# Two tiles to a PSUM bank in the graph convolution and the down projection, and another order of the feed-forward groups

## The chip, the cores and the metric

The kernel runs on one NeuronCore of one Trainium2 chip. The metric is the device time of one execution in microseconds (us). The core has five engines that run side by side, each through its own queue in order: TensorE for matmuls (PE, and PEld for its weight loads), VectorE (DVE), ScalarE (ACT), GpSimd (POOL), and SyncE (SP), which here only issues DMAs. TensorE writes its results to PSUM, which has banks of 512 fp32 values in each of 128 partitions.

## The reference

The input `x` has 32 graphs of 512 nodes with 256 features each; `adj` has a 512 x 512 integer adjacency matrix per graph. Two layers follow, each a graph step and a feed-forward step with residuals. What the change touches is in layer 0:

```python
# graph step (xn = layernorm of x)
h = einsum('bnf,fu->bnu', xn, W_msg)
msg_sum = einsum('bij,biu->bju', a, h)
deg = sum(a, axis=1)
messages = where(deg > 0, msg_sum / maximum(deg, 1), 0)
x = x + relu(einsum('bnf,fu->bnu', xn, W_upd) + messages + bias)

# feed-forward step (xf = layernorm of x, one row per node)
t = max over d of (xf[:, d] + Wt[f, d]) + bt          # 1024 values f per row
trop = s * max_k(t * sl_cvx + of_cvx) + (1 - s) * min_k(t * sl_ccv + of_ccv)
classical = gelu(xf @ Wc + bc)
g = sigmoid(xf @ Wg + bg)
x = x + (g * trop + (1 - g) * classical) @ Wd + bd
```

Layer 1 is an attention over the graph with four heads and a second mixer; nothing in it is changed.

## The kernel before

Layer 0 is `layer0_sorted`. The 32 graphs are handled in four segments of eight. A segment has 8 x 512 = 4096 rows, 32 tiles of 128 rows.

**The graph convolution.** `conv_in(b)` loads a graph, casts its adjacency to floats on POOL (L384), normalizes and transposes it, and makes the messages `h`: for each of four tiles two matmuls into `ph` (L393) and an ACT copy of 256 columns (L395). `conv_out(b)` goes through the four tiles: two matmuls into `pu` (L408), a DVE add of the bias into `u` (L411), four matmuls of the adjacency with `h` into `pm` (L414), whose last column is the degree, then on DVE its maximum with 1, its reciprocal and the scaled sum into `u` (L418 to L420), the relu and residual into `keep` (L422) and the statistics of the next layer norm (L424, L425). Its second half, the tail, normalizes each tile on ACT and finds on DVE a bound, the eight largest values and their places (L439 to L441), counts how many values can matter, and stores rows and values to HBM (`rows_of`, L450).

**The order of rows.** `put_in_order(s)` ranks the 4096 rows of a segment by that count (DVE passes over up to 4096 columns, L493, and small matmuls). Rows with a like count come to lie in the same tile; tile n of a segment needs at most `CAPS[n]` of the 256 features: 24 for the first tile, 9, 7, 6, 5 for the next ones, down to 1 for the last nine.

**The feed-forward groups.** A segment is worked through in NG = 8 groups of four tiles; group g has tiles g, g + 8, g + 16 and g + 24, so group 0 holds the tile that needs 24 features and group 7 is the lightest. `sums(s, g)` gathers the rows of a group (L533), and for each tile gathers a row of `table` (1024 values) for the largest feature (L544) and one for every further feature up to the cap (L578, four buffers); DVE adds the feature's value and takes the maximum (L581, the "row pass", 128 x 1024). Over the caps of its tiles a group makes 27 such passes for g = 0, and 12, 10, 9, 7, 7, 7 and 5 for g = 1 to 7. `mixed(s, g)` runs over eight blocks of 128 outputs: matmuls for `cls` and `gate` (L601) with an ACT function each (L603), the transposed sums `tz` (L608), ACT and DVE passes for the bends of the piecewise function (L614, L615) and three DVE passes that apply the gate (L617 to L619). `down(s, g)` multiplies the result with `wd`: for each of four tiles eight matmuls into `po` (L628) and a DVE add into `xs` (L630), then the group is stored.

**What sets the order.** The functions are generators, and `woven` steps two of them in proportion to given counts. `feed_forwards` runs `mixed` of a group woven with `sums` of the next group; `down` of the group before is issued after the first block of `mixed`. The whole of it is woven with `all_convs`, which works ahead on the convolutions of later segments, and after the last segment on preparations of layer 1. `sums` doesn't begin before its segment is in order. A scheduler then places the instructions on each engine; within an engine they run in that order. The pool of PSUM tiles has four tags of two banks each. `ph`, `pu`, `pm`, `po` and the small matmuls of `put_in_order` share the tag `mm`: each takes the next of its two banks, and waits until the engine that read that bank last is done. Groups come in this order:

```python
groups = [(s, g) for s in range(len(x2s)) for g in reversed(range(NG))]
```

So in each segment the lightest group comes first and the heaviest last.

Of the kernel before, what the change touches and what calls it, by code (L numbers as in the profile page):

```python
# [8 lines left out]
F32 = mybir.dt.float32  # L9
# [4 lines left out]
ALU = mybir.AluOpType  # L14
# [4 lines left out]
P = 128  # L19
N = 512  # L20
D = 256
NT = N // P
DC = D // P
# [3 lines left out]
def deviation(nc, rs, var, eps):  # L27

    nc.gpsimd.tensor_add(rs, var, eps[:, 0:1].to_broadcast(rs.shape))
    nc.gpsimd.tensor_tensor(rs, rs, eps[:, 1:2].to_broadcast(rs.shape), ALU.pow)  # L30
# [66 lines left out]
def layer0_sorted(tc, ident, eps, x, adj, w, x2s, ranks, over, following):  # L97
# [6 lines left out]
    nc = tc.nc  # L104
# [4 lines left out]
    FC = FFN // P  # L109
# [5 lines left out]
    NG = ST // NT  # L115
# [11 lines left out]
    with ExitStack() as ctx:  # L127
        cst = ctx.enter_context(tc.tile_pool(name="c0", bufs=1))
        dr = ctx.enter_context(tc.tile_pool(name="d0", bufs=2, space=DRAM))
        ps = ctx.enter_context(tc.tile_pool(name="p0", bufs=2, space=PSUM))  # L130

        def const(name, shape, src):
            t = cst.tile(shape, F32, tag=name, name=name)
            nc.sync.dma_start(t, src)
            return t

        w_msg = const("w_msg", [P, DC, D], w["W_msg"].rearrange("(c p) u -> p c u", p=P))
        w_upd = const("w_upd", [P, DC, D], w["W_upd"].rearrange("(c p) u -> p c u", p=P))
        bias = const("bias", [P, D], w["bias"].partition_broadcast(P))
# [3 lines left out]
        wd = cst.tile([P, FC, D], F32, tag="wd", name="wd")  # L143
# [34 lines left out]
        sa = aside.enter_context(tc.tile_pool(name="sa", bufs=2, side="right"))  # L178
# [197 lines left out]
        def conv_in(b):  # L376

            xg = sa.tile([P, NT, D], F32, tag="x", name=f"x{b}")
            nc.sync.dma_start(xg, x[b].rearrange("(t p) d -> p t d", p=P))
            a = sa.tile([P, NT, N], F32, tag="adj", name=f"adj{b}", bufs=2)  # L380
            for t in range(NT):
                ai = sa.tile([P, N], I32, tag="adji", name=f"adji{b}_{t}", bufs=2)
                nc.sync.dma_start(ai, adj[b, t * P : (t + 1) * P, :])
                nc.gpsimd.tensor_copy(a[:, t, :], ai)  # L384
            x1T = sa.tile([P, DC, N], F32, tag="x1T", name=f"x1T{b}", bufs=2)
            layer_norm_T(nc, sa, ps, ident, eps, xg, x1T, f"a{b}", pool=True)
            yield
            h = sa.tile([P, NT, D + 1], F32, tag="h", name=f"h{b}", bufs=1)
            nc.gpsimd.memset(h[:, :, D : D + 1], 1.0)
            for t in range(NT):  # L390
                ph = ps.tile([P, N], F32, tag="mm", name=f"ph{b}_{t}")
                for c in range(DC):
                    nc.tensor.matmul(ph[:, :D], x1T[:, c, t * P : (t + 1) * P], w_msg[:, c, :],  # L393
                                     start=c == 0, stop=c == DC - 1)
                nc.scalar.copy(h[:, t, :D], ph[:, :D])  # L395
            held[b] = xg, a, x1T, h
            yield

        def conv_out(b, counts):


            xg, a, x1T, h = held.pop(b)
            keep = sa.tile([P, NT, RW], F32, tag="keep", name=f"keep{b}")
            mv = sa.tile([P, NT, 2], F32, tag="mv", name=f"mv{b}")
            for t in range(NT):
                pu = ps.tile([P, N], F32, tag="mm", name=f"pu{b}_{t}")
                for c in range(DC):
                    nc.tensor.matmul(pu[:, :D], x1T[:, c, t * P : (t + 1) * P], w_upd[:, c, :],  # L408
                                     start=c == 0, stop=c == DC - 1)
                u = sa.tile([P, D], F32, tag="upd", name=f"u{b}_{t}")  # L410
                nc.vector.tensor_add(u, pu[:, :D], bias)  # L411
                pm = ps.tile([P, N], F32, tag="mm", name=f"pm{b}_{t}")
                for i in range(NT):
                    nc.tensor.matmul(pm[:, : D + 1], a[:, i, t * P : (t + 1) * P], h[:, i, :],  # L414
                                     start=i == 0, stop=i == NT - 1)

                deg = sa.tile([P, 1], F32, tag="deg", name=f"deg{b}_{t}")
                nc.vector.tensor_scalar_max(deg, pm[:, D : D + 1], 1.0)  # L418
                nc.vector.reciprocal(deg, deg)
                nc.vector.scalar_tensor_tensor(u, pm[:, :D], deg, u, ALU.mult, ALU.add)  # L420
                x1 = keep[:, t, :D]
                nc.vector.scalar_tensor_tensor(x1, u, 0.0, xg[:, t, :], ALU.max, ALU.add)  # L422
                st = sa.tile([P, 6], F32, tag="ln_st", name=f"stb{b}_{t}", bufs=4)
                nc.vector.bn_stats(st, x1)  # L424
                nc.vector.bn_aggr(mv[:, t, :], st)  # L425
                yield
            rs = sa.tile([P, NT], F32, tag="ln_rs", name=f"rsb{b}", bufs=2)
            deviation(nc, rs, mv[:, :, 1], eps)
            shift = sa.tile([P, NT], F32, tag="ln_shift", name=f"shiftb{b}", bufs=2)
            nc.vector.scalar_tensor_tensor(shift, mv[:, :, 0], -1.0, rs, ALU.mult, ALU.mult)  # L430
            for t in range(NT):
                k, n = keep[:, t, :], b * NT + t
                nc.gpsimd.tensor_copy(k[:, MEAN : MEAN + 1], shift[:, t : t + 1])
                nc.gpsimd.tensor_copy(k[:, MEAN + 1 : MEAN + 2], rs[:, t : t + 1])
                xn = sa.tile([P, D], F32, tag="ln_xn", name=f"xnb{b}_{t}", bufs=3)
                nc.scalar.activation(xn, k[:, :D], AF.Identity, bias=shift[:, t : t + 1], scale=rs[:, t : t + 1])
                rest = sa.tile([P, D], F32, tag="rest", name=f"rest{n}")
                bound = ends[:, 0, n : n + 1]
                nc.vector.tensor_tensor_reduce(rest, xn, low, -1.0, 3e38, ALU.add, ALU.min, bound)  # L439
                nc.vector.max(k[:, VAL : VAL + 8], xn)  # L440
                nc.vector.max_index(k[:, IDX : IDX + 8].bitcast(U32), k[:, VAL : VAL + 8], xn)  # L441


                nc.scalar.activation(rest, xn, AF.Sign, bias=bound, accum_out=counts[:, t : t + 1])
                nc.gpsimd.tensor_copy(k[:, COUNT : COUNT + 1], counts[:, t : t + 1])
                nc.gpsimd.tensor_copy(ends[:, 1, n : n + 1], k[:, VAL : VAL + 1])
                if t + 1 < NT:
                    yield
            rows = rows_of[b // SEG].rearrange("(b t p) w -> b p t w", t=NT, p=P)
            nc.sync.dma_start(rows[b % SEG], keep)  # L450
            yield
# [61 lines left out]
        def convs(s):  # L513
            counts = sa.tile([P, ST], F32, tag="counts", name=f"counts{s}")
            yield from conv_in(s * SEG)
            for i in range(SEG):
                b = s * SEG + i
                after = conv_in(b + 1) if i + 1 < SEG else iter(())
                yield from woven(conv_out(b, counts[:, i * NT : (i + 1) * NT]), 8, after, 2)
            yield from put_in_order(s, counts)  # L520
            placed_segs.add(s)

        def feed_forwards():
# [98 lines left out]

            def down(s, g):
                xg, acc = got.pop((s, g))
                for t in range(NT):
                    po = ps.tile([P, N], F32, tag="mm", name=f"po{s}_{g}_{t}")
                    for f in range(FC):
                        nc.tensor.matmul(po[:, :D], acc[f][:, t * P : (t + 1) * P], wd[:, f, :],  # L628
                                         start=f == 0, stop=f == FC - 1)
                    nc.vector.tensor_add(xg[:, t, :D], xg[:, t, :D], po[:, :D])  # L630
                nc.sync.dma_start(x2s[s].rearrange("(t k p) d -> k p t d", k=NG, p=P)[g], xg[:, :, :D])

            got = {}
            groups = [(s, g) for s in range(len(x2s)) for g in reversed(range(NG))]
            yield from sums(*groups[0])
            for i, now in enumerate(groups):
                steps_ = mixed(*now)
                next(steps_)
                if i:
                    down(*groups[i - 1])  # L640
                yield
                more = sums(*groups[i + 1]) if i + 1 < len(groups) else iter(())
                yield from woven(steps_, 9, more, 8)
            down(*groups[-1])

        def all_convs():
# [20 lines left out]
        for _ in woven(feed_forwards(), NG * 11 + sum(1 + cap // 4 for cap in CAPS), ahead, SEG * 12 + 5):  # L667
            pass
# [1543 lines left out]
```

## Time and profile before

| | |
|---|---|
| time, median of 3 runs | 4689.87 us (4680.16 to 4715.24) |
| the profiled execution | 4695.45 us |
| its span in the profile | 4693.7 us, 56440 instructions |
| TensorE clock granted, mean share of full speed | 0.948 |
| row passes on DVE, L581 | 336, about 1.3 us each |
| down projections on PE, L628 | 456.2 us busy |
| DVE adds of a tile of 256 columns, L411, L630 | 413 ns and 411 ns, 128 of each |
| DVE residual pass of a tile, L422 | 441 ns, 128 of them |
| ACT copy of `h`, L395 | 373 ns, 128 of them |

The profile is one execution on the chip. A row of an engine's groups gives the line, the engine, the operation, what it writes and reads, the count, the busy time in us, the mean in ns, and then how long the engine was idle just before these instructions and what ended that wait. A row of waits says which instruction waited for which, with the total in us, how often, and the longest. A stretch of time is shown with its limits in us from the start of the span. A TensorE record covers part of a matmul only: two records stand for one fp32 matmul.

### The profile page before, as it was taken

To read this page: it belongs to the slowest core of one execution; us is meant where nothing else is said; L and a number is where in the kernel's file an instruction comes from. 1 tells how busy PE (TensorE), PEld (TensorE's weight loads), DVE (VectorE), ACT (ScalarE), POOL (GpSimd) and SP (SyncE) were. 2 spreads that over 40 slices of the span, in tenths; PEclk is the share of its full clock that TensorE was granted. 3 is DMA by queue.
4 is the path that set the end of the run, shared out by engine and by line. 5 is a ranking of instruction groups with operands and counts; after the bars stand their busy time and mean duration, and the time that the engine had idled before them with its cause. 6 is when DMAs were issued, how large, how long until landed. Compare 5 with 4: busy or idle time off the path is not lost. (4 is left out here: it accounts for less than half of the span.)

```text
span 4693.7 us, 56440 instructions
## 1 busy us (share of the span) xinstructions
PE 4097.9 (87%) x19287; PEld 2514.5 (54%) x19287; DVE 3410.9 (73%) x7232; ACT 2310.3 (49%) x4820; POOL 1747.3 (37%) x2027
## 2 busy tenths in 40 slices
PE   5769887889888899879988899999999999999987
PEld 4545554555555565545554355555555555555555
DVE  6667778777787777867777667777777777777773
ACT  2345555455554555546554444544454554444432
POOL 2363445535456444443443322233333233322220
PEclk8889999999999999989999899999999999999998
DMA  4453445535355343554443211111111111111100
GB/s 123 160 173 104 154 133 165 176 105 163 123 162 173 121 142 107 165 186 143 145 159 113 64 46 45 48 46 52 52 53 55 53 55 55 46 55 55 39 14 15
DMA packets 235101, 474.10 MB, mean 101 GB/s; under 512 B 38299, under 2 KB 114075, under 8 KB 234804
## 3 DMA queue, kind: packets, MB, share of 16 engines
q0 software_dynamic: 80256, 282.38, 19.0%
q1 hardware_dynamic: 154548, 188.02, 12.9%
q8 instruction: 154, 2.52, 0.2%
q14 instruction: 143, 1.17, 0.1%
HBM read 413.16 MB, written 57.16 MB: 100 GB/s over the span
## 5 line engine op out<-in xcount | busy, mean ns | idle before, releaser
L601 PE MATMUL clsp<-xnT,wc 128*128 128x512 f32 x1024 | 530.9, 639 | 92.7 <-ACT cls L603 48.5
L601 PE MATMUL gatep<-xnT,wg 128*128 128x512 f32 x1024 | 505.2, 615 | 32.9 <-ACT gate L603 23.4
L628 PE MATMUL po<-wd,acc 128*128 128x256 f32 x2048 | 456.2, 381 | 20.4 <-DVE xs L630 19.9
L628 PEld LDWEIGHTS po<-wd,acc 128*128 128x128 f32 x2048 | 385.9, 190 | 96.3 <-DVE xs L630 31.8
L1186 DVE SCALAR_TENSOR_TENSOR att<-own,other,mask 128x512 f32<-128x512 f32 x512 | 376.3, 757 | 17.9 <-DMA own<-ownd 16.9
L615 DVE SCALAR_TENSOR_TENSOR acc<-past,fld,acc 128x512 f32<-128x512 f32 x448 | 349.5, 784 | 51.7 <-ACT past L614 38.0
L581 DVE SCALAR_TENSOR_TENSOR best<-rows,xs,best 128x1024 f32<-128x1024 f32 x212 | 276.0, 1304 | 124.5 <-ACT best L575 62.5
L601 PEld LDWEIGHTS gatep<-xnT,wg 128*128 128x128 f32 x1024 | 200.3, 199 | 289.5 <-issue 210.6
L614 ACT ACTIVATE past<-tz,fld 128x512 f32<-128x512 f32 x448 | 293.6, 693 | 97.5 <-DVE acc L615 97.1
L601 PEld LDWEIGHTS clsp<-xnT,wc 128*128 128x128 f32 x1024 | 189.8, 202 | 246.6 <-issue 126.4
L1219 PE MATMUL avp<-att,hv 128*64 128x512 f32 x1024 | 309.8, 628 | 3.3 <-DVE att L1186 3.3
L578 POOL DMA_INDIRECT rows<-table,xs x212 | 253.8, 1197 | 109.4 <-DVE best L581 49.5
L414 PE MATMUL pm<-h,adj 128*128 128x257 f32 x1024 | 268.1, 403 | 28.3 <-DVE u L411 18.5
L1307 PE MATMUL lgp<-wsl,x4T 128*128 128x512 f32 x512 | 253.1, 630 | 33.6 <-DVE mask L1058 26.2
L603 ACT ACTIVATE cls<-clsp,fld 128x512 f32<-128x512 f32 x256 | 176.1, 688 | 215.3 <-PE clsp L601 111.0
L1319 PE MATMUL yTp<-sw,x 128*128 128x512 f32 x512 | 244.1, 617 | 36.8 <-DVE sw L1314 29.6
L1127 POOL DMA_INDIRECT x<-x2s,ranks x128 | 141.3, 1104 | 346.9 <-DVE att L1186 128.5
L617 DVE TENSOR_TENSOR acc<-acc,cls 128x512 f32<-128x512 f32 x256 | 180.6, 707 | 94.3 <-ACT acc L610 88.6
L603 ACT ACTIVATE gate<-gatep,fld 128x512 f32<-128x512 f32 x256 | 175.2, 684 | 149.7 <-PE gatep L601 118.2
L610 ACT ACTIVATE acc<-tz,fld 128x512 f32<-128x512 f32 x256 | 199.0, 779 | 96.4 <-PE tz L608 90.8
L533 POOL DMA_INDIRECT xs<-rows_of,order x128 | 146.5, 1144 | 264.6 <-DVE acc L615 118.3
L414 PEld LDWEIGHTS pm<-h,adj 128*128 128x128 f32 x1024 | 201.1, 202 | 77.8 <-DVE u L411 25.6
(597 smaller groups left out, 8999.1 us busy)
## 6 DMA issues: line engine op xcount, KB each, us to landing
adji<-in_adj SPq DMA_DIRECT2D x128, 256.0 KB, 4.5
ai<-in_adj SPq DMA_DIRECT2D x128, 256.0 KB, 2.7
own<-ownd SPq DMA_DIRECT2D x128, 256.0 KB, 3.7
rows_of<-keep SPq DMA_DIRECT2D x32, 550.0 KB, 6.7
x<-in_x SPq DMA_DIRECT2D x32, 512.0 KB, 7.6
x2s<-xs SPq DMA_DIRECT2D x32, 512.0 KB, 2.9
out<-x SPq DMA_DIRECT2D x32, 512.0 KB, 3.2
rows<-table,xs POOLq DMA_INDIRECT x212, 5.4
```

What stands on the lines that cost most here:

```text
L414: nc.tensor.matmul(pm[:, : D + 1], a[:, i, t * P : (t + 1) * P], h[:, i, :], start=i == 0, stop=i == NT - 1)
L578: nc.gpsimd.indirect_dma_start(out=row, out_offset=None, in_=table, in_offset=bass.IndirectOffsetOnAxis(ap=idxs[:, k : k + 1].bitcast(U32) ...
L581: nc.vector.scalar_tensor_tensor(m, row, vals[:, k : k + 1], m, ALU.add, ALU.max)
L601: nc.tensor.matmul(pf, wf[:, c, f * P : (f + 1) * P], xnT[:, c, :], start=c == 0, stop=c == DC - 1)
L603: nc.scalar.activation(o, pf, fn, bias=fld[:, f, bf : bf + 1], scale=1.0 if fn == AF.Gelu else 0.5)
L614: nc.scalar.activation(r, z, AF.Relu, bias=fld[:, f, AT + b : AT + b + 1])
L615: nc.vector.scalar_tensor_tensor(y, r, fld[:, f, CH + b : CH + b + 1], y, ALU.mult, ALU.add)
L628: nc.tensor.matmul(po[:, :D], acc[f][:, t * P : (t + 1) * P], wd[:, f, :], start=f == 0, stop=f == FC - 1)
L1186: nc.vector.scalar_tensor_tensor(e, own[h], other[:, j, h : h + 1], mask[:, j, :], ALU.max, ALU.mult)
L1219: nc.tensor.matmul(pv[q][k * HO : (k + 1) * HO, :], hv[:, j, h, :HO], weighed[b, h, j], start=j == 0, stop=j == NT - 1)
L1307: nc.tensor.matmul(pf, xnT[:, c, t * P : (t + 1) * P], wsl[:, c, :], start=c == 0, stop=c == DC - 1)
L1319: nc.tensor.matmul(py, xn[:, t, c * P : (c + 1) * P], sw[:, t, :], start=t == 0, stop=t == NT - 1)
```

## The change

Three things are changed in `layer0_sorted`:

- `ph` and `pu` hold two tiles of 256 columns side by side in a bank, and one ACT copy, or one DVE add, reads both. `pm` keeps a bank per tile (257 columns). `u` is one buffer of two tiles instead of two of one; the relu with the residual is one pass for two tiles, and the statistics of both follow it. `conv_out` still yields once for each tile.
- `po` holds two tiles, with one DVE add for both.
- The groups begin with group 7 of segment 0; after it come groups 0 to 6 of that segment and then groups 0 to 7 of each further segment.

```diff
-            for t in range(NT):
-                ph = ps.tile([P, N], F32, tag="mm", name=f"ph{b}_{t}")
-                for c in range(DC):
-                    nc.tensor.matmul(ph[:, :D], x1T[:, c, t * P : (t + 1) * P], w_msg[:, c, :],
-                                     start=c == 0, stop=c == DC - 1)
-                nc.scalar.copy(h[:, t, :D], ph[:, :D])
+            for t0 in range(0, NT, 2):
+                ph = ps.tile([P, 2, D], F32, tag="mm", name=f"ph{b}_{t0}")
+                for i in range(2):
+                    t = t0 + i
+                    for c in range(DC):
+                        nc.tensor.matmul(ph[:, i, :], x1T[:, c, t * P : (t + 1) * P], w_msg[:, c, :],
+                                         start=c == 0, stop=c == DC - 1)
+                nc.scalar.copy(h[:, t0 : t0 + 2, :D], ph)
...
-            for t in range(NT):
-                pu = ps.tile([P, N], F32, tag="mm", name=f"pu{b}_{t}")
...
-                u = sa.tile([P, D], F32, tag="upd", name=f"u{b}_{t}")
-                nc.vector.tensor_add(u, pu[:, :D], bias)
-                pm = ps.tile([P, N], F32, tag="mm", name=f"pm{b}_{t}")
...
-                x1 = keep[:, t, :D]
-                nc.vector.scalar_tensor_tensor(x1, u, 0.0, xg[:, t, :], ALU.max, ALU.add)
-                st = sa.tile([P, 6], F32, tag="ln_st", name=f"stb{b}_{t}", bufs=4)
-                nc.vector.bn_stats(st, x1)
-                nc.vector.bn_aggr(mv[:, t, :], st)
-                yield
+            for t0 in range(0, NT, 2):
+                two = slice(t0, t0 + 2)
+                pu = ps.tile([P, 2, D], F32, tag="mm", name=f"pu{b}_{t0}")
...
+                u = sa.tile([P, 2, D], F32, tag="upd", name=f"u{b}_{t0}", bufs=1)
+                nc.vector.tensor_add(u, pu, bias.unsqueeze(1).to_broadcast([P, 2, D]))
+                deg = sa.tile([P, 2], F32, tag="deg", name=f"deg{b}_{t0}")
+                for k in range(2):
+                    t = t0 + k
+                    pm = ps.tile([P, N], F32, tag="mm", name=f"pm{b}_{t}")
...
+                    nc.vector.scalar_tensor_tensor(u[:, k, :], pm[:, :D], deg[:, k : k + 1], u[:, k, :],
+                                                   ALU.mult, ALU.add)
+                    yield
+                nc.vector.scalar_tensor_tensor(keep[:, two, :D], u, 0.0, xg[:, two, :], ALU.max, ALU.add)
+                for t in range(t0, t0 + 2):
+                    st = sa.tile([P, 6], F32, tag="ln_st", name=f"stb{b}_{t}", bufs=4)
+                    nc.vector.bn_stats(st, keep[:, t, :D])
+                    nc.vector.bn_aggr(mv[:, t, :], st)
...
-                for t in range(NT):
-                    po = ps.tile([P, N], F32, tag="mm", name=f"po{s}_{g}_{t}")
...
-                    nc.vector.tensor_add(xg[:, t, :D], xg[:, t, :D], po[:, :D])
+                for t0 in range(0, NT, 2):
+                    po = ps.tile([P, 2, D], F32, tag="mm", name=f"po{s}_{g}_{t0}")
...
+                    nc.vector.tensor_add(xg[:, t0 : t0 + 2, :D], xg[:, t0 : t0 + 2, :D], po)
...
-            groups = [(s, g) for s in range(len(x2s)) for g in reversed(range(NG))]
+
+            groups = [(0, NG - 1)]
+            groups += [(s, g) for s in range(len(x2s)) for g in range(NG) if (s, g) != groups[0]]
```

## The prediction

> **What bounds the kernel now.** I read the page first, then three long stretches, then who TensorE waits for, then one such wait instruction by instruction, then single groups of 512 rows of layer 0. The busy line and the stretches (start:end, length, then busy time of PE, its weight loads, DVE, ACT, POOL, the granted clock, DMA share, GB/s):
>
> ```profile
> PE 4097.9 (87%) x19287; PEld 2514.5 (54%) x19287; DVE 3410.9 (73%) x7232; ACT 2310.3 (49%) x4820; POOL 1747.3 (37%) x2027
> 0.00:338.00 338.00, 212.15 (x873) 161.17 (x874) 217.79 (x804) 116.63 (x261) 124.86 (x320) 0.84 0.50 150
> 338.00:2572.00 2234.00, 1949.26 (x7197) 1236.86 (x7196) 1694.99 (x3259) 1210.82 (x2059) 1025.16 (x1264) 0.95 0.45 145
> 2572.00:4694.00 2122.00, 1936.44 (x11218) 1116.43 (x11218) 1498.11 (x3171) 982.86 (x2501) 597.32 (x444) 0.96 0.16 47
> ```
>
> The first stretch is the graph convolution of segment 0 beside the weight features, the second the 32 feed-forward groups, the third layer 1, which the change doesn't touch. In the second TensorE is busy 87%, idle 285 us, and DVE is at 76%, so neither is free. The waits of TensorE there (total us, times, longest), then two of the first stretch:
>
> ```profile
> PE ph L393 <- DVE xs L630: 58.5, 27, 5.6
> PE clsp L601 <- ACT cls L603: 48.5, 29, 4.8
> PE clsp L601 <- ACT gate L603: 44.0, 23, 8.0
> PE po L628 <- DVE xs L630: 19.9, 25, 1.7
> ...
> PE pm L414 <- DVE u L411: 18.5, 9, 6.9
> PE pu L408 <- DVE u L411: 15.1, 4, 8.2
> ```
>
> The largest single wait is a wait for a bank: messages (`ph`) come right behind the down projections (`po`), both take the two `mm` banks in turn, and the bank comes free only when DVE has added `po` to `xs`. The timeline (start, length, instruction, idle before it and who ended it) shows why DVE is late:
>
> ```profile
> 553.10 1.26 DVE L581 SCALAR_TENSOR_TENSOR best<-rows,xs,best 128x1024 f32<-128x1024 f32 x1
> 557.88 1.28 DVE L581 SCALAR_TENSOR_TENSOR best<-rows,xs,best 128x1024 f32<-128x1024 f32 x1 [3.51 <-DMA rows<-table,xs]
> 559.08 0.41 DVE L630 TENSOR_TENSOR xs<-xs,po 128x256 f32<-128x256 f32 x1
> 559.55 2.08 PE L393 MATMUL ph<-w_msg,x1T 128*128 128x256 f32 x4 [5.59 <-DVE xs L630]
> ```
>
> The add stands in DVE's queue behind row passes, one of which waits 3.51 us for its gather; TensorE stands 5.59 us. Single groups:
>
> ```profile
> 537.00:611.00 74.00, 65.54 (x242) 42.80 (x241) 54.87 (x113) 40.90 (x72) 33.63 (x48) 0.93 0.43 137
> 762.00:863.00 101.00, 78.33 (x312) 48.51 (x311) 85.76 (x142) 48.59 (x81) 67.43 (x58) 0.93 0.64 203
> 1064.00:1131.00 67.00, 61.62 (x241) 40.89 (x240) 52.45 (x111) 40.16 (x71) 29.70 (x45) 1.00 0.42 133
> 1949.00:2047.00 98.00, 69.49 (x232) 37.67 (x231) 79.85 (x122) 42.59 (x66) 59.69 (x60) 0.83 0.65 211
> 2447.00:2502.00 55.00, 47.84 (x161) 28.82 (x160) 46.58 (x59) 28.48 (x43) 31.47 (x23) 0.91 0.61 200
> ```
>
> The first holds the stall above and lasts 74 us; the third, with the same work, waits for such adds 1.4 us in all and lasts 67. The second and fourth run the sums of a heaviest group (27 rows) and are bound by DVE (85% and 81%); the last also runs heavy sums, but without a convolution beside them, and costs nothing.
>
> **What the Trainium skill says.** "TensorE: Matmul & The Clock Gate", What's actually happening: an idle window of about 3.4 us drops TensorE to half clock until it has been busy as long. The trace agrees: 0.93 granted with the 5.59 us stall, 1.00 without. "PSUM — Partial Sum Buffer", Engine vs sequencer instructions: VectorE's queue is strict FIFO; the four timeline lines agree. "VectorE: DVE Perf Modes", The TRN2 errata: a fixed cost per instruction, (N+151)/0.96 ns for an fp32 add, which makes an estimated 691 ns at 512 and 424 at 256; the trace has 707 (gate passes, L617) and 413 (L411). "Perfetto Trace Analysis", Optimizing Scalar/DVE Operations: larger operations help a saturated engine, smaller ones can end a bubble elsewhere; both sides are in play here.
>
> **The change part by part.** *Fewer bank turns.* A convolution took 4 turns of the `mm` banks for `ph` and 8 for `pu` and `pm`; now 2 and 6. A down projection took 4, now 2: the third and fourth `po` no longer wait for an add of the same projection, so the 19.9 us go. In the changed kernel's built order `ph` mostly stands before the down projection, and behind it come `pu` (bank free for 7 us already) and `pm`, which needs the second add. In front of that add, counted from the last gate pass of the group before, DVE held in most groups 8 row passes, 14 passes of the convolution's tail (about 0.35 us from start to start in the timeline) and 4 adds, 8 x 1.28 + 14 x 0.35 + 4 x 0.41 = 16.8 us, against 14.2 us of `po` (7.07 + 7.17). Now it is 7 to 9 row passes and 2 adds, at most 9 x 1.28 + 2 x 0.71 = 12.9 us, in all but about six groups, which keep some of the tail. So DVE reaches the add as TensorE ends, unless a gather is late. Of 78.4 us of such waits I take 59 (three quarters) as gone. Behind them the waits for ACT's `cls` and `gate` banks are next, so a third of it returns: 40 us. The clock adds to it: of the two groups above one is 7 us longer for 5 us more of such waits (6.4 against 1.4), so 2 for the clock; there are some ten groups like it, of whose 20 us I take 10. Together -50; bounds -10 (the wait only changes its name) and -80.
>
> *One pass for two tiles.* `u`, `keep` and `xs`: 64 pairs each. By the page's rows 2 x 413 - 707, 2 x 441 - 736 and 2 x 411 - 707 ns save 119, 146 and 115, x64 = 24 us of DVE; `h`: 2 x 373 - 593 = 153 ns x64 = 10 us of ACT. Spread over 32 groups that is under 1 us each, hidden behind TensorE but for the four DVE-bound groups: -3; bounds -15 and +5. The cost of waiting for both tiles: the first half of a bank is read up to 3.5 us later (8 matmuls), and `pu` passes 0.3 us later; nobody needs them earlier than `pm` or the row store at the end. The single `u` buffer costs nothing: its writer and readers are all DVE, in order. Layer norm statistics come after the second tile, one tile (1.7 us of `pm`) later; the store of `rows_of` waits on the whole image anyway.
>
> *The order of groups.* The heaviest sums (27 rows) stood beside the next-to-last group of each segment, now beside the last one of the segment before, and in segment 0 beside the very first. (a) At the start, 338 to 469 us, two groups took 131 us with DVE at 97. They get 39 rows for 14: 25 x 1.28 + some 6 us of top-value passes = 38, so DVE 135, and at the 0.83 of the DVE-bound pair at 762 to 922 (133 of 160) 162 us: +31. (b) The placement of a segment (one pass of 4.4 us, in all about 12 us of DVE) fell beside the heavy sums, at 1949 even without a convolution: 98 us. Now they are apart: -15 there, 0 for the two middle segments, whose heavy pair has the same DVE sum. (c) The last three groups, 170 us from 2387, become light; at 54 us as the light group at 2333: -8. Sum +8; bounds -20 and +45. POOL's queue gets the same gathers, in another order; each segment's order is ready before its sums in both built orders.
>
> *First stretch.* Its 54 us of waits (the two above, and four smaller ones for `u` and `h`) for `mm` banks belong to TensorE at 63%, beside 45.6 us for layer norm that stay: -10; bounds 0 and -25.
>
> Sum: -50 - 3 + 8 - 10 = -55. The profiled execution took 4695.45 us (span 4693.7, 1.7 around it), 5.6 above the median 4689.87. So 4640 on that execution, **4635** against the median.
>
> **The rivals.** *All of it pays (0.18).* The bank waits go whole (-75, clock included), and early heavy sums spill into the next group at no cost, as at 2447: -20 for the order. With -3 and -2 that gives -100: 4590. Against it: the start has a convolution beside the sums, 2447 had none.
>
> *The wait changes its name (0.14).* `pm` follows the down projection with only 4 matmuls of `pu` between, 1.7 us; if gathers land late (59.1 us of DVE's waits are for them) it waits for the second add as `ph` did. Then only 20 us of `po` waits, 3 and about 3 of the start are gained, against +8: -18, 4672.
>
> *Slower: heavy sums meet convolutions (0.13).* Before, two of four heavy groups had a convolution beside them, now three, the first with the pipeline just filled. If that pair loses what 1949 lost (98 against 57, +41), the pairs in the middle +10 each and (b) and (c) give nothing, the order costs 61; with -10 for the banks it is +51: 4741. It decides where the three pairs together cost more than the banks give.
>
> That the change doesn't do what it says I exclude: the built order shows 2 adds per group and the heavy group second.
>
> **How the numbers follow.** My forecast, 4635, has 0.55, with 4605 to 4665 for its own; about three fifths of it is under 4643. A measurement of this kernel tells about 1% (47 us) from no change. Faster by over 1%: 0.33 + 0.18 = 0.51; slower: the upper half and more of the last case, 0.10; within: 0.39. Range: from 4580, inside the case where all pays, to 4722, inside the slow one.
>
> **What would show it.** Right: waits of `ph`, `po` and `pm` for `xs` together under 30 us, light groups with a convolution at 67 to 70 us and clock near 1.00, the first two groups at 155 to 170 us, the group at the last placement under 70, layer 1 at 2122. Wrong: a new `pm` wait near 58 us, or light groups still at 73; then the row gathers set the pace. Heavy pairs over 175 us would make the last rival right.

## The result and the profile after

The changed kernel took 4619.74 us in the median of 4 runs (4614.30 to 4623.76), the kernel before 4686.46 us beside it: a ratio of 0.9842 as recorded (that of the two medians is 0.9858), with a 95% interval from 0.9818 to 0.9867. That is 67 us faster where 55 were forecast. The profiled execution took 4623.49 us, 72.0 less than the one before. Its busy line and its three stretches, cut at the first `cls` projection and at the end of the last down projection (start:end, length, busy time of PE, weight loads, DVE, ACT, POOL, granted clock, DMA share, GB/s):

```profile
PE 4067.9 (88%) x19287; PEld 2525.4 (55%) x19287; DVE 3379.1 (73%) x7040; ACT 2291.7 (50%) x4756; POOL 1729.5 (37%) x2027
```

```profile
0.00:324.00 324.00, 207.04 (x874) 161.93 (x875) 209.34 (x764) 111.87 (x238) 118.03 (x316) 0.84 0.50 147
324.00:2505.00 2181.00, 1928.64 (x7197) 1248.44 (x7195) 1669.30 (x3108) 1197.75 (x2018) 1013.33 (x1268) 0.95 0.47 149
2505.00:4621.00 2116.00, 1932.26 (x11218) 1115.05 (x11218) 1500.45 (x3171) 982.05 (x2501) 598.15 (x444) 0.97 0.16 48
```

The first stretch is shorter by 14.5 us and the feed-forward groups by 52.6 (2181.4 for 2234.0 at the exact ends). Layer 1, which nothing touches, stands at 2116 for 2121; over all the runs below it lies between 2112.8 and 2121.3, so less than about 9 us in one stage of one profile is not read as a difference. So far this looks like the forecast. The waits of TensorE in the second stretch (total us, times, longest) do not:

```profile
PE pm L422 <- DVE xs L640: 67.3, 16, 8.0
PE clsp L609 <- ACT cls L611: 63.0, 41, 6.3
PE pm L422 <- DVE u L427: 20.2, 9, 6.2
PE ph L395 <- DVE xs L640: 16.0, 2, 8.6
PE clsp L609 <- ACT gate L611: 14.2, 7, 3.0
```

The waits of `po` for the add are gone, as forecast, but `pm` and `ph` together wait 83.3 us for it where `ph` and `po` waited 78.4. In total the wait was not removed; it changed its name. One of them in the timeline (start, length, engine, instruction, idle before it and who ended it), in the group that answers to the one shown of the kernel before:

```profile
545.15 13.98 PE L638 MATMUL po<-wd,acc 128*128 128x256 f32 x64
...
550.00 1.15 ACT L583 ACTIVATE best<-best,xs 128x1024 f32<-128x1024 f32 x1 [5.00 <-DMA best<-table,xs]
...
552.80 5.25 DVE L589 SCALAR_TENSOR_TENSOR best<-rows,xs,best 128x1024 f32<-128x1024 f32 x4 [6.68 <-ACT best L583]
...
557.96 0.68 DVE L640 TENSOR_TENSOR xs<-xs,po 128x512 f32<-128x512 f32 x1
558.96 1.89 PE L413 MATMUL pu<-w_upd,x1T 128*128 128x256 f32 x8
...
559.50 1.28 DVE L589 SCALAR_TENSOR_TENSOR best<-rows,xs,best 128x1024 f32<-128x1024 f32 x1 [0.86 <-DMA rows<-table,xs]
...
562.19 1.28 DVE L589 SCALAR_TENSOR_TENSOR best<-rows,xs,best 128x1024 f32<-128x1024 f32 x1 [1.40 <-DMA rows<-table,xs]
564.06 3.89 DVE L589 SCALAR_TENSOR_TENSOR best<-rows,xs,best 128x1024 f32<-128x1024 f32 x3 [0.58 <-DMA rows<-table,xs]
567.87 0.68 DVE L640 TENSOR_TENSOR xs<-xs,po 128x512 f32<-128x512 f32 x1
...
568.69 2.91 PE L422 MATMUL pm<-h,adj 128*128 128x257 f32 x6 [7.84 <-DVE xs L640]
```

`po` runs from 545.15 to 559.13 and `pu` to 560.85. DVE starts its nine row passes only at 552.80, because ACT's first touch of `best` had waited for a gather; three more gaps of 0.86, 1.40 and 0.58 us between the passes are gathers too. The second add, which frees the bank for `pm`, ends at 568.55. TensorE stands 7.84 us for it. This is no exception: in 12 of the 16 waits of `pm` in the list above DVE had first waited 4.0 to 6.7 us for ACT's `best`, and ACT for a gather. In the group shown of the kernel before DVE waited 3.03 us there.

Some groups of 512 rows in the same view (the columns of the stretches):

```profile
545.00:620.00 75.00, 63.92 (x241) 42.37 (x240) 53.63 (x108) 38.84 (x69) 32.21 (x46) 0.95 0.42 134
828.00:907.00 79.00, 67.95 (x258) 45.71 (x257) 71.33 (x122) 41.76 (x71) 52.33 (x60) 0.96 0.70 227
1201.00:1267.00 66.00, 62.02 (x242) 41.30 (x241) 49.04 (x98) 38.11 (x66) 30.50 (x43) 1.00 0.43 137
1914.00:1974.00 60.00, 51.18 (x212) 31.42 (x211) 47.83 (x84) 34.46 (x54) 21.51 (x27) 0.94 0.46 133
2399.00:2447.00 48.00, 46.65 (x170) 28.47 (x169) 34.14 (x46) 30.41 (x46) 8.08 (x6) 1.00 0.21 66
```

The first holds the stall above and is as long as its like was before. The second runs the heaviest sums, now beside the last group of a segment: 79 us where 101 were. The fourth is the place that took 98 us before, the last one a group at the end of the layer.

To see where the 52.6 us lie, the 32 groups (each from the end of one down projection to the end of the next, the first from the first `cls`) fall into four sorts. The same sums for the experiments stand beside them and are used below; all are us of one profiled execution.

| | before first `cls` | first two groups | three pairs with placement and heavy sums | last three | the other 21 | all 32 |
|---|---|---|---|---|---|---|
| before | 338.5 | 148.4 | 159.4, 160.0, 157.7 | 164.3 | 1444.1 | 2234.0 |
| after | 324.0 | 171.3 | 148.9, 150.6, 138.5 | 141.3 | 1430.9 | 2181.4 |
| order alone | 332.7 | 173.7 | 155.7, 157.0, 139.0 | 141.3 | 1411.6 | 2178.3 |
| convolution's banks alone | 325.0 | 140.6 | 156.9, 156.4, 157.8 | 164.4 | 1415.3 | 2191.3 |
| down projection's bank alone | 338.5 | 146.3 | 159.6, 162.5, 156.9 | 164.4 | 1460.9 | 2250.7 |
| start 20 steps ahead, nothing else | 341.6 | 145.5 | 150.9, 150.5, 142.7 | 166.3 | 1430.6 | 2186.4 |
| that and the convolution's banks | 322.7 | 141.9 | 150.4, 150.2, 150.5 | 166.1 | 1405.6 | 2164.6 |
| new order, start 9 steps ahead | 304.2 | 191.4 | 168.7, 167.3, 140.2 | 140.2 | 1398.9 | 2206.7 |

### The profile page after: what moved, and what is told of

It reads as the page before. It is cut to its first block, busy times and chain, and to the rows that moved or that the text cites. A ratio compares the mean times of both kernels' runs of the same rounds, so it can differ in the third digit from the quotient of the medians.

```text
span 4621.6 us, 56127 instructions
## 1 busy us (share of the span) xinstructions
PE 4067.9 (88%) x19287; PEld 2525.4 (55%) x19287; DVE 3379.1 (73%) x7040; ACT 2291.7 (50%) x4756; POOL 1729.5 (37%) x2027
## 5 line engine op out<-in xcount | busy, mean ns | idle before, releaser
L609 PE MATMUL clsp<-xnT,wc 128*128 128x512 f32 x1024 | 512.1, 621 | 77.3 <-ACT cls L611 63.0
L422 PE MATMUL pm<-h,adj 128*128 128x257 f32 x1024 | 295.5, 435 | 136.3 <-DVE xs L640 67.3
L623 DVE SCALAR_TENSOR_TENSOR acc<-past,fld,acc 128x512 f32<-128x512 f32 x448 | 351.1, 787 | 54.3 <-ACT past L622 45.5
L422 PEld LDWEIGHTS pm<-h,adj 128*128 128x128 f32 x1024 | 212.4, 218 | 194.5 <-issue 106.7
L1284 POOL TENSOR_TENSOR mu<-mu,eps 128x16 f32<-128x16 f32 x32 | 121.3, 3791 | 324.2 <-DVE mu L1283 323.1
```

The lines of the kernel that those rows point to most:

```text
L609: nc.tensor.matmul(pf, wf[:, c, f * P : (f + 1) * P], xnT[:, c, :], start=c == 0, stop=c == DC - 1)
L623: nc.vector.scalar_tensor_tensor(y, r, fld[:, f, CH + b : CH + b + 1], y, ALU.mult, ALU.add)
```

## The experiments

**The parts one by one.** Four kernels, each with one part of the change or all but one. `order_alone` has the new list of groups and nothing else:

```diff
-            groups = [(s, g) for s in range(len(x2s)) for g in reversed(range(NG))]
+            groups = [(0, NG - 1)]
+            groups += [(s, g) for s in range(len(x2s)) for g in range(NG) if (s, g) != groups[0]]
```

> The kernel before with the new order of groups alone. The theory of the prediction (the banks pay, the order costs about 8 us) expects 4690 to 4700 us. The rival that the traces before and after suggest (the bank waits only changed their name, 78.4 us for xs before and 83.3 after, and the gain of 53 us in the feed-forward stretch comes from the heavy sums no longer meeting the placement) expects 4635 to 4650. If both parts are needed together, 4670 to 4690.

`banks_alone` is the changed kernel with the old list:

```diff
-            groups = [(0, NG - 1)]
-            groups += [(s, g) for s in range(len(x2s)) for g in range(NG) if (s, g) != groups[0]]
+            groups = [(s, g) for s in range(len(x2s)) for g in reversed(range(NG))]
```

> The changed kernel with the old order of groups. The theory of the prediction expects 4615 to 4630 us, light groups at 67 to 70 us. The rival expects only the first stretch's 14 us and a few us for the fewer passes: 4660 to 4675, with the heavy pairs still near 160 us and waits for xs still 60 us or more.

`down_alone` has the change's `down` and nothing else, and `conv_alone` the change's loops over `ph`, `pu` and `pm` and nothing else:

```diff
-                for t in range(NT):
-                    po = ps.tile([P, N], F32, tag="mm", name=f"po{s}_{g}_{t}")
...
+                for t0 in range(0, NT, 2):
+                    po = ps.tile([P, 2, D], F32, tag="mm", name=f"po{s}_{g}_{t0}")
...
+                    nc.vector.tensor_add(xg[:, t0 : t0 + 2, :D], xg[:, t0 : t0 + 2, :D], po)
```

> The kernel before with only the down projections two tiles to a bank. The theory of the prediction puts the larger half of the 50 us here, 20 for the po waits and some 15 of the ph waits: about 4650 us. The rival expects the 19.9 us of po waits to go and ph to wait longer for an add that comes later: 4675 to 4690, first stretch as before (338 us).

> The kernel before with only messages and updates two tiles to a bank. The theory of the prediction expects some 25 us from fewer bank turns and 10 from the first stretch: about 4650 us. The rival expects the first stretch's 14 us and little else: 4670 to 4680, with the waits for xs moved from ph to pm.

Measured, each against the kernel before:

| kernel | median us | ratio, 95% interval |
|---|---|---|
| order alone | 4629.81 | 0.9880 [0.9865, 0.9896] |
| both banks, old order | 4655.39 | 0.9925 [0.9909, 0.9942] |
| down projection's bank alone | 4696.18 | 1.0014 [1.0005, 1.0023] |
| convolution's banks alone | 4632.74 | 0.9873 [0.9856, 0.9890] |

Against 4690.57 us in that set the order gives 61 us, the convolution's banks 58, and the down projection's bank costs 6. Put beside the convolution's banks in the old order it costs 23 (4655.39 against 4632.74). Its waits show it; first the kernel with that part alone, then the one with both banks:

```profile
PE ph L393 <- DVE xs L632: 87.8, 19, 9.5
```

```profile
PE ph L395 <- DVE xs L640: 103.6, 19, 10.2
```

The kernel before had 58.5 us there, the longest 5.6, and 19.9 us of `po`; `conv_alone`, to be set against the second line, has 45.1 and 13.9. (Each list is of one execution; that of `down_alone` took 4705.44 us, 9 more than its median.) With two tiles to a bank `po` waits no more, but all of it and more comes back at `ph`: the one add that frees the bank is also the one that must get past DVE's row passes. The Trainium skill, "Perfetto Trace Analysis", Optimizing Scalar/DVE Operations, says that breaking up an operation can let work end sooner where its engine isn't saturated but holds up another. That agrees with this run: DVE is busy 76% of the groups' time, and the kernel with the smaller adds is the faster one by 6 us.

In `conv_alone` the waits for `xs` are not the larger part of the gain either. They fall by 19 us, to 59.0, while the waits of layer norm's transposes (`lnpa`) for ACT fall by 35, from 40.1 to 4.7. How these hang on the banks no run shows.

The order alone has already renamed the wait. Its waits of the three kinds:

```profile
PE pm L414 <- DVE xs L630: 34.2, 15, 5.4
PE po L628 <- DVE xs L630: 22.9, 26, 3.3
...
PE ph L393 <- DVE xs L630: 7.9, 4, 2.1
```

They sum to 65.0, so 13 of the 78.4 are gone, but the groups gained 56. What fell most is the waits for ACT's `cls` and `gate`, from 125 us to 62; some for `h` and `u` came in their place. The 56 are not one thing. By the table the first two groups lose 25, the three pairs gain 26 (19 of it at the last placement), the last three gain 23 and the other 21 gain 32.

**Do the parts add?** If they did, order and convolution's banks would give 119 us together. `order_conv` is the changed kernel with the old `down`, `order_down` the one with the old `ph`, `pu` and `pm`.

> The change without its down projections: the new order with messages and updates two tiles to a bank, the down projection one tile to a bank as before. Theory (the down projection's larger pass is what costs, as in the run of the convolution's banks with and without it, 23 us): 4585 to 4605, the waits of TensorE for xs under 60 us. Rival (the order and the convolution's banks gain from the same stalls, so together they stop at what the full change has): 4612 to 4630. If all parts were independent: 4572.

> The new order with the down projections two tiles to a bank, the convolution as before. Theory (the larger pass of the down projection costs some 6 to 20 us whatever the order): 4636 to 4650, with pm waiting for xs 60 us or more. Rival (in the new order the messages stand before the down projection, so its larger pass delays nobody and saves its turns): 4610 to 4625.

They measured 4623.72 us (0.9865, 0.9843 to 0.9887) and 4618.27 us (0.9856, 0.9835 to 0.9877), against 4686.25. The theory fell in both. Under the new order the convolution's banks are worth 6 us, less than the spread of that kernel's own runs (4614.62 to 4640.80), and the down projection's bank no longer costs: it is 11 us better than without. The full change, 4619.74, can't be told from either. So with the order taken first, it brings nearly all, and the banks, either or both, some 10 us. Taken the other way round, both banks bring 35 us (4655.39) and the order 36 more. The parts don't add, so no single split of the 67 us is the right one.

Where the convolution's banks went under the new order can in part be read from the waits. `order_conv` (the profiled execution, 4640.80 us, is the slowest of its five):

```profile
PE pm L422 <- DVE u L427: 40.0, 12, 6.1
PE po L636 <- DVE xs L638: 39.1, 33, 4.1
PE pm L422 <- DVE xs L638: 24.8, 12, 3.9
```

The waits of `pm` for its own earlier pass (`u`, L427) were 14.1 us with the order alone. One of them:

```profile
727.17 0.15 DVE L425 TENSOR_SCALAR deg<-pm 128x1 f32<-128x1 f32 x1
727.24 0.74 DVE L623 SCALAR_TENSOR_TENSOR acc<-past,fld,acc 128x512 f32<-128x512 f32 x1
727.90 1.40 DVE L626 SCALAR_TENSOR_TENSOR acc<-gate,acc 128x512 f32<-128x512 f32 x1
...
731.15 0.15 DVE L426 RECIPROCAL deg<-deg 128x1 f32<-128x1 f32 x1
731.26 0.69 DVE L625 TENSOR_TENSOR acc<-acc,cls 128x512 f32<-128x512 f32 x1
731.87 0.48 DVE L427 SCALAR_TENSOR_TENSOR u<-pm,deg,u 128x256 f32<-128x256 f32 x1
...
732.49 2.05 PE L422 MATMUL pm<-h,adj 128*128 128x257 f32 x4 [6.11 <-DVE u L427]
```

The bank's first reader, `deg`, runs at 727.17, its last one at 731.87; between them stand passes of the feed-forward (L623, L625, L626). It is the same wait a third time: a bank that DVE reads late because other work stands ahead in its queue.

**Taking the add off DVE.** `down_act` is the changed kernel with this in `down`, so that no row pass stands before the bank:

```diff
-                    nc.vector.tensor_add(xg[:, t0 : t0 + 2, :D], xg[:, t0 : t0 + 2, :D], po)
+                    for i in range(2):
+                        part = acc[FC - 2 + i][:, t0 * P : (t0 + 2) * P]
+                        nc.scalar.copy(part, po[:, i, :])
+                        nc.gpsimd.tensor_add(xg[:, t0 + i, :D], xg[:, t0 + i, :D], part)
```

> The changed kernel, with the bank of the down projection emptied by ACT (two copies into a dead part of acc) and the sum into xs made by POOL from there, so that DVE's queue no longer stands before the bank. Theory (pm waits because DVE reaches the add late, behind its row passes): the 84 us of waits for xs fall to under 30 us for ACT's copy in its place, and the time to 4575 to 4600. Rival (the wait changes its name once more, to ACT's queue or POOL's): 4610 to 4640, with a wait of pm for acc or for the next u near 50 us or more.

It measured 4629.05 us (0.9882, 0.9861 to 0.9903), 9 us more than the changed kernel. The 83.3 us of waits for `xs` are gone from its list in the same stretch, and these head it:

```profile
PE clsp L609 <- ACT cls L611: 102.6, 47, 10.8
PE pm L422 <- DVE u L427: 40.9, 12, 6.6
PE pm L422 <- DVE u L416: 24.2, 10, 4.6
```

They were 63.0, 20.2 and 7.8. The time and the waits are the rival's: 83 us of one wait were taken away, 77 came back under these three names. Not all of the 77 need be the same wait under a new name: the 128 copies give ACT 47 us of work that it didn't have, and the wait that grew most, by 40 us, is for ACT's `cls`.

**What in the order pays.** `order_mid` puts the heaviest group fifth in all segments, with the old banks:

```diff
-            groups = [(s, g) for s in range(len(x2s)) for g in reversed(range(NG))]
+            groups = [(s, g) for s in range(len(x2s)) for g in (7, 6, 5, 4, 0, 3, 2, 1)]
```

> The kernel before with one line changed: in all four segments the heaviest group is taken fifth (7, 6, 5, 4, 0, 3, 2, 1), so its sums meet neither the placement of a segment nor the first groups. Theory (the order of the change gains because the heaviest sums no longer fall together with the placement, and loses 23 us at the very first group): the groups that took 98 us fall to 70 to 77, the first stays at 75, the heavy ones in mid-segment take 75 to 85: 4600 to 4625. Rival (what gains is that a heavy sum meets the last group of a segment, where TensorE waits anyway, or that the order ascends): 4660 to 4690, with a group of about 95 in mid-segment.

It measured 4660.35 us (0.9948, 0.9933 to 0.9964): 26 us, less than half of what the change's order gives. By the sorts of the table its three pairs take 152.2, 151.0 and 133.6, which is 40 less than before, so heavy sums and placement do cost each other something. But the other 21, which now hold the heavy sums, take 31 more; the last three take 15 less. The theory has the pairs right and forgot that the heavy sums cost where they go: where a convolution runs beside it, the group in mid-segment takes 86 to 88 us (from one down projection's start to the next).

In the change's order the messages stand ahead of the down projection, in the old one behind it. That has nothing to do with banks: the heavy first group has more steps, and so pulls the convolution forward. `phase_alone` does that to the kernel before by one number, `phase_conv` does it to `conv_alone`, and `order_back` and `conv_back` pull it back in `order_alone` and `order_conv` (9 in place of 16):

```diff
-    LEAD = 16
+    LEAD = 20
```

> The kernel before with one number changed: the convolution starts 20 steps ahead of the feed-forward groups in place of 16, so that in the built order messages stand ahead of the down projection, as they do in the change, with the old order and old banks. Theory (what the new order gains in the light groups comes from this shift, not from the order of the sums itself): 4650 to 4665, ph waiting for xs under 10 us, pm waiting for xs over 30. Rival (the shift only renames the wait, and the gain is the sums'): 4680 to 4695 with the same renaming.

> Messages and updates two tiles to a bank in the old order, the convolution started 20 steps ahead in place of 16. Without the shift these banks gave 58 us. Theory (in the shifted place the larger banks give nothing, as under the new order, where they gave 6): within 15 us of the shift alone, 4640 to 4665. Rival (the banks pay wherever the messages stand, and it is the new order that leaves them nothing): 4605 to 4630.

> The new order with the old banks, the convolution started only 9 steps ahead, so that messages stand behind the down projection again, as before. Theory (the shift is about half of what the order gained): 4650 to 4670, ph waiting for xs over 40 us. Rival (the order pays by the sums alone): 4622 to 4640.

> The new order with messages and updates two tiles to a bank, the old down projection, and the convolution started 9 steps ahead in place of 16, so that messages stand behind the down projection. Theory (the banks pay where the messages stand behind the down projection): 50 to 60 us under the run with the old banks in this place, 4590 to 4615. Rival (banks and order gain from the same stalls whatever the place): 4615 to 4640.

The medians, with those from above, all against the kernel before (4686 to 4691 in the three sets):

| | old banks | convolution's banks |
|---|---|---|
| old order, start 16 ahead (messages behind `down`) | 4690.57 | 4632.74 |
| old order, start 20 ahead (messages ahead of it) | 4644.47, 0.9905 [0.9887, 0.9923] | 4601.81, 0.9820 [0.9799, 0.9841] |
| new order, start 16 ahead (messages ahead of it) | 4629.81 | 4623.72 |
| new order, start 9 ahead (messages behind it) | 4638.42, 0.9898 [0.9879, 0.9917] | 4619.59, 0.9861 [0.9841, 0.9882] |

The shift alone, one number, gives 45 us in the old order. The waits for `xs` do not just change their name there, they mostly go:

```profile
PE po L628 <- DVE xs L630: 22.3, 30, 2.2
PE pm L414 <- DVE u L420: 16.1, 16, 1.5
...
PE pm L414 <- DVE xs L630: 7.9, 9, 2.0
```

With `ph` not in the list and 30.2 us for `po` and `pm` together, this is what the prediction had wanted from the banks. The timeline of `phase_alone` shows how:

```profile
1054.96 10.75 PE L628 MATMUL po<-wd,acc 128*128 128x256 f32 x48
...
1060.32 1.28 DVE L581 SCALAR_TENSOR_TENSOR best<-rows,xs,best 128x1024 f32<-128x1024 f32 x1 [5.50 <-ACT best L575]
...
1069.72 0.60 PE L608 MATMUL tz<-ident,best 128*128 128x128 f32 x4
1070.15 0.38 PE L557 MATMUL xsp<-ident,xn 128*128 128x128 f32 x2
1070.37 1.88 PE L601 MATMUL clsp<-xnT,wc 128*128 128x512 f32 x4
...
1072.09 1.88 PE L601 MATMUL gatep<-xnT,wg 128*128 128x512 f32 x4
1072.09 0.42 DVE L630 TENSOR_TENSOR xs<-xs,po 128x256 f32<-128x256 f32 x1
...
1074.24 1.03 PE L408 MATMUL pu<-w_upd,x1T 128*128 128x256 f32 x4
```

DVE isn't earlier: it waits 5.50 us for `best`, and its last add ends after the last `po` by 4.3 us in the mean of the first 22 groups, as in the kernel before (4.4). But TensorE has other work meanwhile. Behind 17 of these 22 down projections stand matmuls of the feed-forward (`cls`, `gate` and transposes), which take no `mm` bank, and the next `mm` taker, `pu`, comes 4.4 us later. In the kernel before, in the changed one and in `order_alone` a taker stands within 1.0 us behind 17 to 19 of the 22. So "messages ahead of `down`" is not the same place in the old order and in the new one.

The theory that the order pays by this shift falls with `order_back`: with the messages behind `down` again the order still gives 51 us (its expectation had 4650 or more, and over 40 us for `ph` where 32.2 came). A start 9 steps ahead also moves work out of the first stretch, which is 34 us shorter, into the first two groups, which are 43 longer than before. In the 30 groups behind these the order gains 81 us at 16 steps and still 70 at 9. And the theory that the banks pay only behind `down` falls with `phase_conv`: there they give 43 on top of the shift. Their gain goes with the order: banks of the convolution give 58 and 43 in the old one, 6 and 19 in the new one. Order, shift and banks each give 45 to 61 alone; with the order, no other part adds more than 19.

One number falls in every version that gains 45 us or more: TensorE's idle time in the feed-forward groups. It was 285 us; it is 241 with the order, 251 with the shift, 254 with the convolution's banks, 253 in the full change, 246 in `phase_conv`, 264 to 267 in the two versions pulled back, whose first stretch is 34 to 46 us shorter instead because fewer steps stand there. Below 241 only `order_down` comes (234). A wait that all of them keep is the one for ACT's `cls` and `gate`, 62 us with the order alone to 151 in `conv_back`. That they all draw on the same idle time, and so can't add, fits this, but it is argued and not shown by a run of its own. It is not the whole either: TensorE's busy time in the groups falls too, from 1949 us to 1937 with the order and to 1919 in `phase_conv`.

`phase_conv`, old order and old down projection, is the fastest of all. Its stretches and two of its groups (same columns):

```profile
0.00:323.00 323.00, 208.98 (x887) 163.27 (x888) 214.64 (x766) 115.11 (x243) 126.25 (x324) 0.85 0.53 157
323.00:2487.00 2164.00, 1918.33 (x7183) 1219.47 (x7181) 1665.29 (x3170) 1198.48 (x2013) 996.75 (x1260) 0.96 0.46 149
...
381.00:447.00 66.00, 61.86 (x241) 40.62 (x241) 48.91 (x107) 38.95 (x67) 29.75 (x45) 1.00 0.42 137
447.00:513.00 66.00, 61.90 (x241) 40.69 (x240) 50.77 (x108) 39.48 (x69) 29.16 (x45) 1.00 0.42 136
```

Light groups with a convolution take 66 us at full clock, as the forecast had it for the changed kernel. Its 5 runs (4596.19 to 4613.42) lie below the 4 of the changed kernel, but were not made beside them, and the two ratios' intervals overlap.

## Why the prediction came out right, and where it was wrong

The time lies inside the forecast's own range, 15 us under its middle of 4635. That is luck: the sum came right by two large errors that cancel. The banks were to give 63 us with the first stretch and the passes, and give 35 in the old order and some 10 in the new one; the order was to cost 8 and gives 61 alone and 36 on top of the banks.

*Fewer bank turns, -50: wrong.* The step that failed is "So DVE reaches the add as TensorE ends". Its count was right: nine row passes and two adds stand before the bank in the timeline above. It let them start with the down projection. Here they start 7.65 us later (545.15 to 552.80), since DVE waits for ACT's `best` and that for a gather, and they have 2.84 us of gathers between them: 7.65 + 11.70 of passes + 1.36 of adds + 2.84 = 23.6 us against 15.9 of `po` and `pu`. The working named the late gather as an exception and priced it at a quarter of the waits; in 12 of the 16 waits of `pm` one held up DVE's start. It also put nothing between the down projection and `pm` but `pu`; in `phase_alone`, where 4.4 us of other work stand there, such waits mostly don't arise. The rival in which the wait changes its name had the mechanism, its place (`pm`) and nearly its size: 67.3 us. It missed the total because it, too, priced the order as a loss.

*The part of the change that was held for its benefit split in two.* In the old order the convolution's banks give 58 us and the down projection's bank costs 6 to 23. The prediction costed the wait for both tiles at nothing ("the first half of a bank is read up to 3.5 us later"), with no other work of TensorE named for the case that the one add is late. `down_alone` shows that cost.

*One pass for two tiles, -3: the durations right, the -3 not tested.* The passes fell from 413 to 672 for two (`u`), 441 to 747 (`keep`), 411 to 681 (`xs`) and on ACT 373 to 577 ns (`h`): 27.5 us of DVE and 10.9 of ACT, where 24 and 10 were forecast. The estimate from "VectorE: DVE Perf Modes", The TRN2 errata, 691 ns for 512 columns, stands between the two adds and `keep`. No run prices them apart from the banks.

*The order, +8: wrong in sign and outside its bounds (-20 to +45).* Alone it gives -61. Term by term, from the table: (a) the first two groups, +31 forecast, +25 measured (+20 between the starts of their down projections, as the forecast had it); (b) -15 at the last placement and 0 at the other two, measured -19, and -4 and -3, too small to be read as differences; (c) the last three, -8 forecast, -23 measured: it was priced with a group of 10 row passes and 54 us, and the groups that come to stand there have 5 to 7 and take 43 to 50. What was missing is a term: the other 21 groups gain 32. The working took the order as a matter of sums alone, and did see in the built order that `ph` had moved ahead of the down projection, but booked that under the banks. The runs don't settle what it is. The shift in the old order brings 13 of the other 21 and 33 of the pairs (`phase_alone`); but in the new order with the start pulled back the other 21 gain 45 and the pairs 1 (`order_back`).

*First stretch, -10: the size nearly right (-14.5; -13.5 with the convolution's banks alone), the reason not shown.* The waits that were to go are there: `pm` for `u` takes 31.3 us where it took 18.5, and all waits for `u` and `h` 55 where they took 58. What fell is TensorE's busy time (212 to 207) and the wait for layer norm (45.6 to 38.6).

*The signs to watch.* Waits for `xs` under 30: 83.3. The new `pm` wait near 58, named as the mark of failure: 67.3. Light groups at 67 to 70: 64 to 78. The first two groups at 155 to 170 by the starts of their down projections: 149. The group at the last placement under 70: 60. The first three speak against the mechanism, though the time came out as forecast.

*Open.* Why the convolution's banks give 43 to 58 us in the old order and 6 to 19 in the new one. The stall at L427 shows one way in which the gain goes. To put these passes ahead of the feed-forward's in DVE's queue with nothing else moved was not tried, nor was other work put behind the down projection in the changed kernel, as `phase_alone` has it. Why the waits for `cls` and `gate` halve with the order alone (62 us) and stand at 122 in `order_back` is open too. The start by 20 steps also moves the placement against the heavy sums, so its gain is not the messages' place alone.

## What to carry to other kernels

A wait for a buffer that two banks share among several producers belongs to the slow reader, not to the producer that is named: ask when that reader's queue can start, not only how much stands in it, and what other work the waiting engine has until then; and expect the wait at the next taker when the present one moves. Measure the parts of a change apart and together: three parts here were worth 61, 58 and -6, and 67 in all. Before banks are repacked, try the one number that sets how two streams of work are interleaved; here it was worth 45 us alone.

## What was not expected

- A larger pass made the wait for it longer: with one add of 681 ns in place of two of 411, and nothing else changed, the waits for `xs` rose from 78.4 to 87.8 us, in one profile of each.
- A wait taken away came back almost whole: 83.3 us of waits for DVE's add, moved to ACT and POOL, returned as 77 us at `cls` and `u`, though part of that may be ACT's added work.
- The granted clock of a group did not follow the length of its longest stall alone: 0.95 with one of 7.84 us here, 0.93 with one of 5.59 us before, and 1.00 with one of 3.2 us before (the group from 922). Groups whose longest wait was 2.0 us or less ran at 0.98 to 1.00 in both.
